# A transformer block with exact fp32 products: the FFN's down products taken from three float32r matmuls, and each FFN sum completed inside one PSUM bank

## The chip, the cores and the metric

The kernel runs on one core of a Trainium2 chip. The time is that of one execution on the device, in microseconds (us). A core has five engines that run side by side, each working through its own queue in order: TensorE (PE) multiplies matrices, VectorE (DVE) and ScalarE (ACT) work element by element, GpSimd (POOL) does the same on SBUF alone, and SyncE (SP) issues the DMAs. Matmul results land in PSUM, which has eight banks of 128 x 512 fp32.

## What is computed

One block over x of 2048 tokens x 512 features: a layer norm, causal attention with 16 heads of 32, and a gated feed-forward network (FFN) of width 4096 on the same normalized input. The FFN's weights are 4-bit codes with a scale for each block of 32.

```python
xn = layernorm(x)
# attention: qkv, causal softmax, output projection with w_o
Wg, Wu, Wd = dequant(gate), dequant(up), dequant(down)
gate, up = xn @ Wg.T, xn @ Wu.T              # 2048 x 4096 each
gelu = tanh(0.7978845608 * (gate + 0.044715 * gate**3)) * gate * 0.5 + gate * 0.5
out = x + attention(xn) + (gelu * up) @ Wd.T
```

## The kernel before

Attention comes first and takes about 855 us. Then the output projection adds into sixteen fp32 accumulators `acc` (128 tokens x 512), and the same loop splits the normalized tokens `xnT` for the FFN. Then the FFN runs.

*Splitting.* A float32r matmul is made exact by cutting each fp32 number into a high part (its upper bits, taken with a mask, `HIGH`) and the low rest. A product of two split numbers is the sum of high x high, low x low and one "mixed" matmul, whose operands are `high * SPLIT - low` on each side; the constants `HIGH_SCALE` and `MIXED_SCALE` bring the sums together. `TRUE` undoes the scale that the decoding of codes leaves.

*Weights.* The FFN's 4096 rows are handled as 8 groups `g` of 4 chunks `j` of 128 rows. For every chunk there are three pieces of weights: gate (m = 0), up (m = 1) and half of a down pair (m = 2). `load_words` (L553) loads the codes and scales of a piece with one DMA and eight DMAs on SP's queue. `piece` (L571) decodes it: five VectorE passes of 128 x 256 (L582 to L600) and two GpSimd multiplies by the scales. For a down piece (L601) that is all: the result goes straight to the fp32 tiles `wd`. A gate or up piece is then split: a VectorE mask for `high` (L625), a GpSimd subtraction for the low part (L626), two ScalarE passes (L627, L628) and a second GpSimd subtraction (L629). This second half, the "rest", is handed out only after the next piece's first four steps.

*Who hands it out.* `weights` (L649) is a generator over all pieces; each `yield` carries an estimate in us. `advance(us)` (L677) takes steps until its budget is spent, `need` (L686) takes steps until a tile exists, and `limit` says how many pieces may have been made so far. So the order on VectorE, GpSimd and ScalarE is fixed by where `advance` and `need` are called. Every engine works in the order in which the code issues; `tc.manual_schedule()` keeps it.

*FFN slots.* The loop at L833 runs over g, j and the four token blocks b in the order 1, 2, 3, 0: 128 slots. `gate_and_up` (L785) makes in each slot twelve matmuls for gate and twelve for up (`products`, L770: high, low and mixed for each of four k), each sum in two PSUM banks. `combine` (L765) copies one bank with a scale to SBUF on ScalarE and adds the other on VectorE. ScalarE applies the gelu, VectorE multiplies gate and up into `inter`. After each of the two groups of twelve, `down` (L809) takes one tile of 128 tokens from a list and adds two fp32 matmuls for it, over the chunks j - 1 and j. An fp32 matmul shows as two MATMUL records. `add` (L825) adds the result to `acc` on VectorE with the factor `TRUE`. The list is filled after every second chunk, so down products trail by up to eight slots, and the `inter` tiles have ten buffers.

*Buffers.* `xnT` of all token blocks is one pool (`norm`) on the right side of SBUF, closed before the FFN. The FFN's pools on the left are, in order, `lm` (split tokens), `acc`, `wd`, `stage`, `deq`, `gu`. The output projection's weights `wo` use two of the four `gu` tiles. A tile that is put where an older one lay waits for that one's last reader.

Of the kernel before, what the change touches and what calls it, by code (L numbers as in the profile page):

```python
# [34 lines left out]
BF16 = mybir.dt.bfloat16  # L36
# [29 lines left out]
HIGH_SCALE = (1.0 + SPLIT) * TRUE  # L66
MIXED_SCALE = -TRUE / SPLIT
# [7 lines left out]
def block_kernel(  # L75
# [12 lines left out]
    const = ctx.enter_context(tc.tile_pool(name="const", bufs=1))  # L88

    ident = const.tile([P, P], F32, tag="ident", name="ident")  # L90
    make_identity(nc, ident)

    mask_qk = const.tile([P, TB], F32, tag="mask_qk", name="mask_qk")
    nc.vector.memset(mask_qk[:, : TB - P], 0.0)
    make_causal_mask(nc, mask_qk[:, TB - P :], mask_val=MASKED)
    ident_h = const.tile([P, P], BF16, tag="ident_h", name="ident_h")
    nc.vector.tensor_copy(ident_h, ident)
    ones_h = const.tile([P, P], BF16, tag="ones_h", name="ones_h")
    nc.vector.memset(ones_h, 1.0)
    ones = const.tile([P, D], F32, tag="ones", name="ones")  # L100
    nc.vector.memset(ones, 1.0)

# [6 lines left out]
    norm_stack = ExitStack()  # L109
    norm = norm_stack.enter_context(tc.tile_pool(name="norm", bufs=1, side="right"))  # L110

    xnT = [norm.tile([P, NK, TB], F32, tag=f"xnT{b}", name=f"xnT{b}") for b in range(NTB)]


    with (
        tc.manual_schedule(),
        tc.tile_pool(name="small", bufs=4) as small,
# [11 lines left out]
    ):  # L129

# [410 lines left out]
    wdp = ctx.enter_context(tc.tile_pool(name="wd", bufs=2, reuse_waits="tile"))  # L541
# [27 lines left out]
    gu, wd = {}, {}  # L569

    def piece(g, m, j, staged):  # L571

        key = f"{g}_{m}_{j}"
        pk, sc = staged  # L580
        code = tp.tile([P, W], I32, tag="code", name=f"code{key}")
        nc.vector.tensor_scalar(code, pk, 0xFF, None, ALU.bitwise_and)  # L582
        yield 0.29
        spread = tp.tile([P, W], I32, tag="spread", name=f"spread{key}")
        nc.vector.scalar_tensor_tensor(
            spread, code, 12, code, ALU.logical_shift_left, ALU.bitwise_or
        )
# [12 lines left out]
        nc.vector.tensor_tensor(mag, y, spread, ALU.bitwise_or)  # L600
        if m == 2:  # L601

            cols = slice((j % 2) * W, (j % 2 + 1) * W)
            for nib in range(2):
                c = 2 * (j // 2) + nib
                if (g, c) not in wd:
                    wd[g, c] = wdp.tile([P, H], F32, tag=f"wd{nib}", name=f"wd{g}_{c}")
                codes = mag16.rearrange("p (n nib) -> p nib n", nib=2)[:, nib]
                nc.gpsimd.tensor_tensor(wd[g, c][:, cols], codes, sc, ALU.mult)
            yield 0.43  # L610
            return

        w = tp.tile([P, NK, P], F32, tag="w", name=f"w{key}")
        for c in range(2):
            nc.gpsimd.tensor_tensor(  # L615
                w[:, 2 * c : 2 * c + 2],
                mag16.rearrange("p (c n nib) -> p c nib n", c=2, nib=2)[:, c],
                sc[:, :P].unsqueeze(1).to_broadcast([P, 2, P]),
                ALU.mult,
            )  # L620
        yield 0.43
        yield None
        parts = gup.tile([P, 3, NK, P], F32R, tag="gu", name=f"gu{key}")
        high = tp.tile([P, NK, P], F32, tag="high", name=f"high{key}")
        nc.vector.tensor_scalar(high.bitcast(I32), w.bitcast(I32), HIGH, None, ALU.bitwise_and)  # L625
        nc.gpsimd.tensor_tensor(parts[:, 1], w, high, ALU.subtract)  # L626
        nc.scalar.activation(parts[:, 2], high, AF.Copy, scale=SPLIT)  # L627
        nc.scalar.copy(parts[:, 0], high)  # L628
        nc.gpsimd.tensor_tensor(  # L629
            parts[:, 2], parts[:, 2].bitcast(F32), parts[:, 1].bitcast(F32), ALU.subtract  # L630
        )
        gu[g, m, j] = parts
        yield 0.43


    pieces = [(0, 0, 0), (0, 1, 0), (0, 2, 0)]
    for g in range(NG):
        for j in range(0, NC, 2):
            pieces += [(g, 0, j + 1), (g, 1, j + 1), (g, 2, j + 1)]
            h, i = (g, j + 2) if j + 2 < NC else (g + 1, 0)  # L640
            if h < NG:
                pieces += [(h, 0, i), (h, 1, i), (h, 2, i)]
# [6 lines left out]
    def weights():  # L649
# [3 lines left out]
        while True:  # L653
            if made < limit[0]:
# [11 lines left out]
                if key[1] < 2:  # L666
                    rest = ops
# [7 lines left out]
    budget, limit = [0.0], [3]  # L675
# [43 lines left out]
    with tc.manual_schedule():  # L719
# [15 lines left out]
        for n, t in enumerate(order):  # L735
# [13 lines left out]
            if n >= 4:  # L749
                token_high(ORDER[n // 4 - 1], n % 4)  # L750
            if n >= 3:
# [5 lines left out]
        norm_stack.close()  # L757


        ip = ctx.enter_context(  # L760
            tc.tile_pool(name="inter", bufs=10, side="right", reuse_waits="tile")
        )
        ep = ctx.enter_context(tc.tile_pool(name="elem", bufs=2, side="right", reuse_waits="tile"))

        def combine(ps, dst, name):  # L765
            t = ep.tile([P, TB], F32, tag="t", name=f"t{name}")
            nc.scalar.activation(t, ps[0], AF.Copy, scale=HIGH_SCALE)  # L767
            nc.vector.scalar_tensor_tensor(dst, ps[1], MIXED_SCALE, t, ALU.mult, ALU.add)  # L768

        def products(g, m, j, b):  # L770

            ps = [bank(f"gu{g}_{m}_{j}_{b}_{i}") for i in range(2)]
            parts = gu[g, m, j]
            for k in range(NK):
                for dst, i, mov, start, stop in (
                    (ps[0], 0, xh[b, k], k == 0, False),
                    (ps[0], 1, lm[b][:, 0, k], False, k == NK - 1),
                    (ps[1], 2, lm[b][:, 1, k], k == 0, k == NK - 1),
                ):
                    nc.tensor.matmul(dst, lhsT=parts[:, i, k], rhs=mov, start=start, stop=stop)  # L780
            return ps

        inters = {}

        def gate_and_up(g, j, b):  # L785
            name = f"{g}_{j}_{b}"
            need(lambda: (g, 0, j) in gu and (g, 1, j) in gu)
            ps = products(g, 0, j, b)
            down()
            gate = ep.tile([P, TB], F32, tag="gate", name=f"gate{name}")  # L790
            combine(ps, gate, f"g{name}")
            nc.scalar.activation(gate, gate, AF.Gelu_apprx_tanh)
            advance(0.5)
            add()
            ps = products(g, 1, j, b)
            down()
            advance(0.8)
            inter = ip.tile([P, TB], F32, tag="inter", name=f"inter{name}")
            combine(ps, inter, f"u{name}")
            nc.vector.tensor_tensor(inter, gate, inter, ALU.mult)  # L800
            inters[g, j, b] = inter
            if j % 2 == 1:
                downs.extend((g, j, 4 * b + i) for i in range(4))
            add()
            advance(1.4)

        downs, adds = [], []

        def down():  # L809

            if not downs:
                return
            g, j, t = downs.pop(0)
            po = bank(f"pd{g}_{j}_{t}")
            for c in (j - 1, j):
                nc.tensor.matmul(  # L816
                    po,
                    lhsT=inters[g, c, t // 4][:, (t % 4) * P : (t % 4 + 1) * P],
                    rhs=wd[g, c],
                    start=(c == j - 1),  # L820
                    stop=(c == j),
                )
            adds.append((g, j, t, po))

        def add():  # L825
            if not adds:
                return
            g, j, t, po = adds.pop(0)
            nc.vector.scalar_tensor_tensor(acc[t], po, TRUE, acc[t], ALU.mult, ALU.add)  # L829
            if (g, j) == (NG - 1, NC - 1):  # L830
                nc.sync.dma_start(out=out[t * P : (t + 1) * P, :], in_=acc[t])
# [6 lines left out]
        while downs:  # L838
            down()
            add()  # L840
# [53 lines left out]
```

## Time and profile before

| | |
|---|---|
| median of 3 runs | 2074.04 us (2071.06 to 2079.86) |
| the profiled execution | 2072.73 us, span 2071.0 us |
| TensorE busy in the span | 2034.8 us |
| VectorE, ScalarE, GpSimd busy | 1174.1, 740.6, 451.3 us |
| mean granted TensorE clock | 0.998 of full |
| gate and up matmuls (L780), 3072 | 640.0 + 503.3 us busy |
| down matmuls (L816), 1024 records | 479.6 us busy |

The spans of neighbouring matmuls overlap, since a matmul starts before the one before it has drained. Busy time of a group therefore counts shared time once for one of them, and a matmul's "mean ns" is longer than its place in the queue; the distance from start to start is what it costs. The clock is granted in steps of half and full speed.

### The profile page before, as it was taken

How to read it: one execution, taken by the hardware profiler on the slowest of the kernel's cores; microseconds unless marked ns; L12 is line 12 of the kernel's file. 1: busy time of each engine (PE TensorE's matmuls, PEld its weight loads, DVE VectorE, ACT ScalarE, POOL GpSimd, SP SyncE). 2: the span in 40 equal slices, each digit the busy share in tenths (PEclk: the TensorE clock that was granted, in tenths of full speed). 3: DMA queues.
4: the chain of work that ended last, by engine and by line, in shares of the span. 5: the costliest groups of instructions: out<-in, count | busy, mean ns of one | idle time of the engine just before them, and what ended most of it. 6: DMA issues, size and time to landing. Idle time of an engine off the chain costs nothing.

```text
span 2071.0 us, 28569 instructions
## 1 busy us (share of the span) xinstructions
PE 2034.8 (98%) x10560; PEld 1067.8 (52%) x10560; DVE 1174.1 (57%) x2354; ACT 740.6 (36%) x1624; POOL 451.3 (22%) x700
## 2 busy tenths in 40 slices
PE   7999999999999999999999999999999999999999
PEld 3433233332333222356666666666666666666665
DVE  5657665557555730496556465555556565555553
ACT  2113565456545577423222222222222222222221
POOL 0000021111111120353323122232313222232310
PEclk9999999999999999999999999999999999999999
DMA  3000000000000000300000000000000000000002
GB/s 122 0 11 31 1 1 1 1 1 1 1 1 1 2 2 1 97 14 26 22 16 21 16 20 20 20 20 17 22 17 18 19 20 19 20 20 16 21 3 81
DMA packets 54941, 39.63 MB, mean 19 GB/s; under 512 B 14737, under 2 KB 47505, under 8 KB 54673
## 3 DMA queue, kind: packets, MB, share of 16 engines
q1 hardware_dynamic: 54800, 37.81, 6.2%
q8 instruction: 83, 1.36, 0.3%
q14 instruction: 58, 0.47, 0.1%
HBM read 33.55 MB, written 4.19 MB: 18 GB/s over the span
## 4 chain that ended last, share of the span: by engine, by line
PE 93%; DVE 3%; ACT 2%; issue 1%; POOL 1%; DMA 0%; DVEq 0%; POOLq 0%; ACTq 0%
PE gu L780 33%; PE pd L816 21%; PE av L342 12%; PE ps_s L205 9%; PE ps_qk L161 6%; PE ps_t L279 4%; PE ps_t L294 3%; PE ps_v L444 3%; ACT prob L308 1%; PE po L738 1%; PE pm L260 0%; POOL lm L705 0%; PE ptx L433 0%; DVE highx L704 0%; DVE sums L362 0%
## 5 line engine op out<-in xcount | busy, mean ns | idle before, releaser
L780 PE MATMUL gu<-lm,gu 128*128 128x512 f32 x2048 | 640.0, 393 | 2.3 <-DVE gate L768 1.2
L780 PE MATMUL gu<-xh,gu 128*128 128x512 f32 x1024 | 503.3, 491 | 1.2 <-ACT tg L767 1.2
L816 PE MATMUL pd<-wd,inter 128*128 128x512 f32 x1024 | 479.6, 592 | 0.6 <-DVE inter L800 0.6
L780 PEld LDWEIGHTS gu<-lm,gu 128*128 128x128 f32 x2048 | 385.1, 188 | 141.3 <-issue 59.3
L229 DVE TENSOR_REDUCE tops<-ps_s 128x1 f32<-128x512 f32 x384 | 243.8, 682 | 157.3 <-PE ps_s L205 137.1
L342 PE MATMUL av<-prob,v 128*32 128x512 f32 (+3 forms) x1280 | 290.3, 542 | 3.7 <-DVE sums L362 2.8
L205 PE MATMUL ps_s<-qk,qk 32*128 32x512 f32 (+3 forms) x1280 | 291.2, 576 | 0.0
L342 PE MATMUL av<-prob,ones 128*32 128x512 f32 (+3 forms) x1280 | 290.3, 542 | 0.0
L816 PEld LDWEIGHTS pd<-wd,inter 128*128 128x128 f32 x1024 | 193.7, 189 | 149.1 <-issue 128.2
L294 PE MATMUL ps_t<-qk,qk 32*128 32x512 f32 (+3 forms) x1280 | 263.6, 535 | 0.0
L308 ACT ACTIVATE prob<-ps_t 128x512 f32<-128x512 f32 x384 | 205.8, 597 | 154.5 <-PE ps_t L294 153.2
L780 PEld LDWEIGHTS gu<-xh,gu 128*128 128x128 f32 x1024 | 192.8, 188 | 94.1 <-issue 58.6
L768 DVE SCALAR_TENSOR_TENSOR gate<-gu,tg 128x512 f32<-128x512 f32 x128 | 88.5, 691 | 231.5 <-ACT tg L767 231.4
L615 POOL TENSOR_TENSOR w<-mag,sc 128x256 f32<-128x256 f16 x128 | 98.2, 788 | 541.9 <-DVE mag L600 541.9
L768 DVE SCALAR_TENSOR_TENSOR inter<-gu,tu 128x512 f32<-128x512 f32 x128 | 88.5, 691 | 218.8 <-ACT tu L767 218.8
L767 ACT ACTIVATE tg<-gu 128x512 f32<-128x512 f32 x128 | 76.1, 594 | 358.5 <-PE gu L780 358.5
L829 DVE SCALAR_TENSOR_TENSOR acc<-pd,acc 128x512 f32<-128x512 f32 x256 | 175.4, 685 | 41.2 <-PE pd L816 41.2
L224 DVE CUSTOM_DVE_ANT_0 ps_s<-ps_s,mask_qk 128x128 f32<-128x128 f32 (+3 forms) x256 | 120.8, 517 | 100.2 <-PE ps_t L294 55.7
L767 ACT ACTIVATE tu<-gu 128x512 f32<-128x512 f32 x128 | 76.3, 596 | 269.8 <-PE gu L780 269.8
L342 PEld LDWEIGHTS av<-prob,v 128*32 128x32 f32 x1280 | 49.4, 108 | 200.9 <-issue 160.2
L319 POOL TENSOR_SCALAR_AFFINE_SELECT prob<-prob 128x256 f32<-128x256 f32 x128 | 52.0, 406 | 432.3 <-ACT prob L318 385.6
L626 POOL TENSOR_TENSOR gu<-w,high 128x512 fp32r<-128x512 f32 x64 | 85.6, 1337 | 238.7 <-DVE high L625 236.3
(75 smaller groups left out, 1965.0 us busy)
## 6 DMA issues: line engine op xcount, KB each, us to landing
pk<-packed SPq DMA_DIRECT2D x96, 128.0 KB, 2.1
sc<-scales SPq DMA_DIRECT2D x512, 8.0 KB, 1.6
x<-x SPq DMA_DIRECT2D x16, 256.0 KB, 3.5
acc<-x SPq DMA_DIRECT2D x16, 256.0 KB, 4.1
sc<-scales SPq DMA_DIRECT2D x256, 16.0 KB, 1.7
out<-acc SPq DMA_DIRECT2D x16, 256.0 KB, 2.0
wqk<-w_qk SPq DMA_DIRECT2D x4, 512.0 KB, 3.6
wv<-w_v SPq DMA_DIRECT2D x1, 1024.0 KB, 6.7
```

The costliest lines, as they stand in the source:

```text
L161: nc.tensor.matmul(ps, lhsT=w[:, k, which, :], rhs=xnT[b][:, k, :], start=(k == 0), stop=(k == NK - 1),)
L205: nc.tensor.matmul(ps[:, :w], lhsT=qT[p // 2, qb][rows, i * P : (i + 1) * P], rhs=kT[p // 2, c][rows, :w], start=True, stop=True,)
L224: nc.vector.tensor_tensor_reduce(ps[:, :w], ps[:, :w], mask_qk[:, TB - w :], 1.0, MASKED, ALU.add, ALU.max, top,)
L229: nc.vector.tensor_reduce(top, ps[:, :w], AX.X, ALU.max)
L294: nc.tensor.matmul(ps[:, c0:], lhsT=kT[p // 2, kt // 4][rows, (kt % 4) * P : (kt % 4 + 1) * P], rhs=qT[p // 2, qb][rows, c0:], start=False ...
L308: nc.scalar.activation(prob[:, h, :], ps, AF.Exp)
L342: nc.tensor.matmul(av[D * h : D * (h + 1), c0:], lhsT=v[kt // 4][:, kt % 4, D * head : D * (head + 1)] if h < 2 else ones, rhs=prob[:, h % ...
L767: nc.scalar.activation(t, ps[0], AF.Copy, scale=HIGH_SCALE)
L768: nc.vector.scalar_tensor_tensor(dst, ps[1], MIXED_SCALE, t, ALU.mult, ALU.add)
L780: nc.tensor.matmul(dst, lhsT=parts[:, i, k], rhs=mov, start=start, stop=stop)
L816: nc.tensor.matmul(po, lhsT=inters[g, c, t // 4][:, (t % 4) * P : (t % 4 + 1) * P], rhs=wd[g, c], start=(c == j - 1), stop=(c == j),)
L829: nc.vector.scalar_tensor_tensor(acc[t], po, TRUE, acc[t], ALU.mult, ALU.add)
```

## The change

1. A down piece is split like a gate or up piece. Its tile `wd` now holds three float32r parts for a pair of chunks; a last ScalarE pass scales the low part (`ready` counts the finished halves of a pair). The list of pieces is made anew: down pieces are made one pair ahead.
2. The down product of a slot's `inter` is made for that chunk alone, in the next slot: `inter` is split into three parts, then for each of four token tiles two matmuls (high, low), a ScalarE rescale of the bank in place, and later one mixed matmul into the same bank. VectorE adds the bank to `acc`, now four times a slot.
3. Gate and up sums use one bank each: eight matmuls, a ScalarE rescale in place, then four mixed matmuls into it. `combine` goes; the gelu and the multiplication read PSUM with a scale.
4. `advance` is called once a slot, with 2.2, where it was called with 0.5, 0.8 and 1.4.
5. Pools: `const` closes with attention, `norm` becomes four pools that close one by one, and `wd` opens only when two of them have.

```diff
-HIGH_SCALE = (1.0 + SPLIT) * TRUE
-MIXED_SCALE = -TRUE / SPLIT
+HIGH_SCALE = -(1.0 + SPLIT) * SPLIT
+SUM_SCALE = -TRUE / SPLIT
...
-    wdp = ctx.enter_context(tc.tile_pool(name="wd", bufs=2, reuse_waits="tile"))
...
+        if m == 2:
+            pair = (g, j // 2)
+            if pair not in wd:
+                wd[pair] = wdp[0].tile([P, 2, 3, H], F32R, tag="wd", name=f"wd{g}_{j // 2}")
+                ready[pair] = 0
+            cols = slice((j % 2) * W, (j % 2 + 1) * W)
+            parts = [wd[pair][:, :, i, cols] for i in range(3)]
+            w, high = (t.rearrange("p (c k) n -> p c (k n)", c=2) for t in (w, high))
+        else:
+            gu[g, m, j] = gup.tile([P, 3, NK, P], F32R, tag="gu", name=f"gu{key}")
+            parts = [gu[g, m, j][:, i] for i in range(3)]
+        nc.gpsimd.tensor_tensor(parts[1], w, high, ALU.subtract)
+        nc.scalar.activation(parts[2], high, AF.Copy, scale=SPLIT)
+        nc.scalar.copy(parts[0], high)
         nc.gpsimd.tensor_tensor(
-            parts[:, 2], parts[:, 2].bitcast(F32), parts[:, 1].bitcast(F32), ALU.subtract
+            parts[2], parts[2].bitcast(F32), parts[1].bitcast(F32), ALU.subtract
         )
         yield 0.43
+        if m == 2:
+            nc.scalar.activation(parts[1], parts[1].bitcast(F32), AF.Copy, scale=1.0 / SPLIT)
+            ready[pair] += 1
...
+    pieces = [(0, 0, 0), (0, 1, 0), (0, 2, 0), (0, 2, 1)]
+    for n in range(NG * NC):
+        g, j = divmod(n + 1, NC)
+        if g < NG:
+            pieces += [(g, 0, j), (g, 1, j)]
+        g, j = divmod(2 * (n // 2 + 1) + n % 2, NC)
+        if g < NG:
+            pieces.append((g, 2, j))
...
-                if key[1] < 2:
-                    rest = ops
+                rest = ops
...
+        def high_and_low(g, m, j, b):
+            ps = bank(f"gu{g}_{m}_{j}_{b}")
+            parts = gu[g, m, j]
+            for k in range(NK):
+                for i, mov in ((0, xh[b, k]), (1, lm[b][:, 0, k])):
+                    nc.tensor.matmul(ps, lhsT=parts[:, i, k], rhs=mov, ...)
+            nc.scalar.activation(ps, ps, AF.Copy, scale=HIGH_SCALE)
+            return ps
+        def mixed(g, m, j, b, ps):
+            for k in range(NK):
+                nc.tensor.matmul(ps, lhsT=gu[g, m, j][:, 2, k], rhs=lm[b][:, 1, k], start=False, ...)
+        def gate_and_up(g, j, b, finish):
+            need(lambda: (g, 0, j) in gu and (g, 1, j) in gu)
+            gate_sum = high_and_low(g, 0, j, b)
+            up_sum = high_and_low(g, 1, j, b)
+            mixed(g, 0, j, b, gate_sum)
+            gate = ep.tile([P, TB], F32, tag="gate", name=f"gate{name}")
+            nc.scalar.activation(gate, gate_sum, AF.Gelu_apprx_tanh, scale=SUM_SCALE)
+            next(finish, None)
+            advance(2.2)
+            mixed(g, 1, j, b, up_sum)
+            inter = ep.tile([P, TB], F32, tag="inter", name=f"inter{name}")
+            nc.vector.scalar_tensor_tensor(inter, up_sum, SUM_SCALE, gate, ALU.mult, ALU.mult)
+            parts = ip.tile([P, 3, TB], F32R, tag="parts", name=f"parts{name}")
+            high = ep.tile([P, TB], F32, tag="hi", name=f"hi{name}")
+            nc.vector.tensor_scalar(high.bitcast(I32), inter.bitcast(I32), HIGH, None, ALU.bitwise_and)
+            nc.scalar.copy(parts[:, 0], high)
+            nc.gpsimd.tensor_tensor(parts[:, 1], inter, high, ALU.subtract)
+            next(finish, None)
+            return down(g, j, b, parts, high)
+        def down(g, j, b, parts, high):
+            nc.vector.scalar_tensor_tensor(
+                parts[:, 2], high, SPLIT, parts[:, 1].bitcast(F32), ALU.mult, ALU.subtract
+            )
+            need(lambda: ready.get((g, j // 2)) == 2)
+            w = wd[g, j // 2][:, j % 2]
+            sums = []
+            for i in range(4):
+                po = bank(f"pd{g}_{j}_{b}_{i}")
+                for part in range(2):
+                    nc.tensor.matmul(po, lhsT=parts[:, part, i * P : (i + 1) * P], rhs=w[:, part], ...)
+                nc.scalar.activation(po, po, AF.Copy, scale=HIGH_SCALE)
+                sums.append(po)
+            yield
+            for i, po in enumerate(sums):
+                nc.tensor.matmul(po, lhsT=parts[:, 2, i * P : (i + 1) * P], rhs=w[:, 2], start=False, ...)
+                t = 4 * b + i
+                nc.vector.scalar_tensor_tensor(acc[t], po, SUM_SCALE, acc[t], ALU.mult, ALU.add)
...
         for g in range(NG):
             for j in range(NC):
                 for b in ORDER:
-                    limit[0] = min(3 * (NC * g + j + 2), 3 * NC * NG)
-                    gate_and_up(g, j, b)
+                    limit[0] = min(4 + 3 * (NC * g + j + 1), 3 * NC * NG)
+                    finish = gate_and_up(g, j, b, finish)
```

The generator `finish` holds the down product of the slot before: its first `next` issues the split's last part, the eight matmuls and the rescales, its second the mixed matmuls and the accumulations.

More of the change, by code (lines that the diff above doesn't have):

```diff
@@ L108, in block_kernel @@
     ]
[L109 to L112 removed]
+    norms, xnT = {}, {}
+    for b in reversed(ORDER):
+        norms[b] = ExitStack()
+        norm = norms[b].enter_context(tc.tile_pool(name=f"norm{b}", bufs=1, side="right"))
+        xnT[b] = norm.tile([P, NK, TB], F32, tag="xnT", name=f"xnT{b}")
     with (
         tc.manual_schedule(),
+        tc.tile_pool(name="const", bufs=1) as const,
         tc.tile_pool(name="small", bufs=4) as small,
@@ L610, in piece @@
[L610 to L620, printed above, removed]
+                nc.gpsimd.tensor_tensor(
+                    w[:, 2 * nib : 2 * nib + 2].rearrange("p k n -> p (k n)"), codes, sc, ALU.mult
+                )
+        else:
+            for c in range(2):
+                nc.gpsimd.tensor_tensor(
+                    w[:, 2 * c : 2 * c + 2],
+                    mag16.rearrange("p (c n nib) -> p c nib n", c=2, nib=2)[:, c],
+                    sc[:, :P].unsqueeze(1).to_broadcast([P, 2, P]),
+                    ALU.mult,
+                )
@@ L621, in piece @@
         yield 0.43
         yield None
-        parts = gup.tile([P, 3, NK, P], F32R, tag="gu", name=f"gu{key}")
         high = tp.tile([P, NK, P], F32, tag="high", name=f"high{key}")
         nc.vector.tensor_scalar(high.bitcast(I32), w.bitcast(I32), HIGH, None, ALU.bitwise_and)
-        nc.gpsimd.tensor_tensor(parts[:, 1], w, high, ALU.subtract)
-        nc.scalar.activation(parts[:, 2], high, AF.Copy, scale=SPLIT)
-        nc.scalar.copy(parts[:, 0], high)
+        if m == 2:
[6 more added lines that the diff above has]
+            w, high = (t.rearrange("p (c k) n -> p c (k n)", c=2) for t in (w, high))
+        else:
+            gu[g, m, j] = gup.tile([P, 3, NK, P], F32R, tag="gu", name=f"gu{key}")
+            parts = [gu[g, m, j][:, i] for i in range(3)]
@@ L674, in block_kernel @@
     work = weights()
-    budget, limit = [0.0], [3]
+    budget, limit = [0.0], [2]
     def advance(us):
@@ L756, in block_kernel @@
             token_high(ORDER[-1], k)
[L757 to L768, printed above, removed]
@@ L770, in products @@
-        def products(g, m, j, b):
-            ps = [bank(f"gu{g}_{m}_{j}_{b}_{i}") for i in range(2)]
+        for b in ORDER[2:]:
+            norms[b].close()
+        ep = ctx.enter_context(tc.tile_pool(name="elem", bufs=1, side="right", reuse_waits="tile"))
+        ip = ctx.enter_context(tc.tile_pool(name="ip", bufs=2, side="right", reuse_waits="tile"))
+        def high_and_low(g, m, j, b):
+            ps = bank(f"gu{g}_{m}_{j}_{b}")
             parts = gu[g, m, j]
             for k in range(NK):
[L775 to L780, printed above, removed]
-            return ps
@@ L783, in block_kernel @@
-        inters = {}
-        def gate_and_up(g, j, b):
+                for i, mov in ((0, xh[b, k]), (1, lm[b][:, 0, k])):
+                    nc.tensor.matmul(
+                        ps,
+                        lhsT=parts[:, i, k],
+                        rhs=mov,
+                        start=(k == 0 and i == 0),
+                        stop=(k == NK - 1 and i == 1),
+                    )
+            nc.scalar.activation(ps, ps, AF.Copy, scale=HIGH_SCALE)
+            return ps
+        def mixed(g, m, j, b, ps):
+            for k in range(NK):
+                nc.tensor.matmul(
+                    ps,
+                    lhsT=gu[g, m, j][:, 2, k],
+                    rhs=lm[b][:, 1, k],
+                    start=False,
+                    stop=(k == NK - 1),
+                    skip_group_check=True,
+                )
@@ L793, in gate_and_up @@
[L793 to L807, printed above, removed]
@@ L816, in down @@
                 nc.tensor.matmul(
                     po,
[L818 to L821, printed above, removed]
-                )
[L823 to L831, printed above, removed]
+                    lhsT=parts[:, 2, i * P : (i + 1) * P],
@@ L833, in block_kernel @@
+                    rhs=w[:, 2],
+                    start=False,
+                    stop=True,
+                    skip_group_check=True,
+                )
+                t = 4 * b + i
+                nc.vector.scalar_tensor_tensor(acc[t], po, SUM_SCALE, acc[t], ALU.mult, ALU.add)
+                if (g, j) == (NG - 1, NC - 1):
+                    nc.sync.dma_start(out=out[t * P : (t + 1) * P, :], in_=acc[t])
+        finish = iter(())
         for g in range(NG):
@@ L835, in block_kernel @@
                 for b in ORDER:
-                    limit[0] = min(3 * (NC * g + j + 2), 3 * NC * NG)
-                    gate_and_up(g, j, b)
-        while downs:
-            down()
-            add()
+                    limit[0] = min(4 + 3 * (NC * g + j + 1), 3 * NC * NG)
+                    finish = gate_and_up(g, j, b, finish)
+        for _ in finish:
+            pass
 def _arranged(a):
```

68 lines of the change are left out of this document (32 added, 36 removed).

## The prediction

> **What bounds the kernel now.** I read the page's table of engines first, then the chain of waits in the feed-forward part, then single instructions there.
>
> ```profile
> PE 2034.8 (98%) x10560; PEld 1067.8 (52%) x10560; DVE 1174.1 (57%) x2354; ACT 740.6 (36%) x1624; POOL 451.3 (22%) x700
> ```
>
> TensorE (PE) is full and nothing else is near it. The chain of waits over 20 us of the feed-forward part, in order of time (start, length, what):
>
> ```profile
> by line: PE gu L780 62.5%; PE pd L816 38.6%
> ...
> 1403.11 2.78 PE gu L780 x12
> 1405.88 1.72 PE pd L816 x4
> 1407.60 2.78 PE gu L780 x12
> 1410.38 1.72 PE pd L816 x4
> ```
>
> No other engine is on the chain. Twelve float32r matmuls take 2.78 us, 0.232 each; the four records of two fp32 down matmuls take 1.72, so 0.86 for each fp32 matmul. One slot (a chunk j and token block b) is 2 x 4.50 = 9.0 us, and 128 slots are 1152 us of the 2071. Only what changes TensorE's work, or makes it wait, counts. Now the other engines over one weight piece (start, length, engine, line; a bracket is idle time before it):
>
> ```profile
> 1416.53 1.35 POOL L626 TENSOR_TENSOR gu<-w,high 128x512 fp32r<-128x512 f32 x1 [5.72 <-DVE high L625]
> ...
> 1417.96 1.29 POOL L629 TENSOR_TENSOR gu<-gu 128x512 fp32r<-128x512 f32 x1
> 1418.07 1.46 DVE L585 SCALAR_TENSOR_TENSOR spread<-code 128x256 int32<-128x256 int32 x1
> ...
> 1422.40 0.42 DVE L625 TENSOR_SCALAR high<-w 128x512 int32<-128x512 int32 x1
> ...
> 1422.85 0.63 ACT L627 ACTIVATE gu<-high 128x512 fp32r<-128x512 f32 x1 [3.03 <-DVE high L625]
> 1422.96 1.33 POOL L626 TENSOR_TENSOR gu<-w,high 128x512 fp32r<-128x512 f32 x1 [2.16 <-DVE high L625]
> 1423.39 0.61 ACT L628 CAST gu<-high 128x512 fp32r<-128x512 f32 x1
> ...
> 1424.38 1.27 POOL L629 TENSOR_TENSOR gu<-gu 128x512 fp32r<-128x512 f32 x1
> 1425.61 1.43 POOL L609 TENSOR_TENSOR wd<-mag,sc 128x256 f32<-128x256 f16 x2
> ```
>
> ScalarE (ACT) passes are 0.6 us and start 0.53 apart when queued; GpSimd (POOL) steps are 1.3 us, a pair of scale multiplies 1.43; VectorE (DVE) hands to POOL after about 0.13. Last, TensorE's clock where it was idle: windows of 3.41 us, with its busy time first and the granted clock third from the end:
>
> ```profile
> 840.83:844.25 3.42, 1.48 (x15) 0.48 (x12) 0.52 (x1) 3.38 (x11) 0.81 (x2) 1.00 0.00 0
> 844.25:847.66 3.41, 3.09 (x16) 0.68 (x16) 3.35 (x5) 2.48 (x10) 1.37 (x4) 0.50 0.00 0
> 851.08:854.49 3.41, 1.63 (x28) 0.47 (x24) 1.07 (x2) 2.35 (x7) 1.84 (x5) 1.00 0.38 118
> 854.49:857.90 3.41, 3.04 (x4) 1.49 (x5) 3.38 (x5) 0.00 (x0) 1.31 (x3) 0.50 0.08 19
> ...
> 936.41:939.82 3.41, 2.17 (x9) 1.31 (x8) 0.86 (x3) 2.65 (x6) 3.33 (x4) 1.00 0.16 41
> 939.82:943.24 3.42, 3.42 (x17) 2.78 (x16) 2.20 (x4) 1.82 (x4) 0.51 (x1) 1.00 0.15 39
> ```
>
> Busy for 1.48 or 1.63 of 3.41 us, the next window has half the clock (four fp32 records start in the second, where about eight do at full clock); busy for 2.17, it keeps it.
>
> **The sum of matmuls.** Out go 512 fp32 matmuls: 512 x 0.86 = 440. In come 3 x 4 per slot, 1536 float32r matmuls of the shape of the gate and up ones: 1536 x 0.232 = 356. Gate and up keep their 24. Term: -84 us (bounds -78 and -88, a pitch 0.004 off). A slot becomes 36 x 0.232 = 8.35 us: gate pairs until 1.86, up pairs 3.71, gate mixed 4.64, eight matmuls of the previous slot's down product 6.50, up mixed 7.42, its four mixed ones 8.35.
>
> **Work on the other engines, per slot.** ACT: the two copies with scale become rescales in place (0.6 each), the gelu stays, four rescales of down sums and one copy of `high` come in, 0.6 each; with 7 weight passes per four slots (4 before) about 5.9 of 8.35 us. DVE: two combines and a product (2.1) become one product, one mask and one mixed part (0.69 + 0.42 + 0.78), and accumulations go from two to four (+1.37); with weights about 6.6. POOL: one subtraction (1.34) per slot, and two more per down piece; about 4.5. Each sum fits under 8.35, so by load alone TensorE would hide it all. Down's rescales and weight passes stand in queues, though, so I followed the order in which the new code issues them. DMAs of weights stay: 96 pieces, the same bytes.
>
> **Where the queue does not fit.** Per chunk, three weight pieces are spread by the budget of 2.2 per slot. The third slot (b = 3) draws, in this order: the rest of the up piece, the scale multiplies of the down piece, and at once the down piece's own rest, ending in a rescale of its low part. ACT, all in issue order, has behind that rescale the copy of `parts[:, 0]` and then the next slot's gate rescale, for which TensorE waits. Times from the slot's first matmul:
> - gelu starts when the gate mixed matmuls have drained (4.64 + 0.19; a matmul takes 0.40 at a pitch of 0.23) = 4.83; four down rescales start at 5.39, 5.92, 6.45, 6.98; the up piece's `high x SPLIT` pass runs 7.51 to 8.13.
> - POOL's second subtraction of that piece needs it: 8.25 to 9.54. Only then come the down piece's multiplies, 9.50 to 10.93.
> - DVE's mask `high`: 10.97 to 11.39. POOL's subtractions: 11.53 to 12.86 and 12.95 to 14.24.
> - ACT's rescale of the low part reads what the second subtraction reads, so it waits for it: 14.28 to 14.88; copy, start 14.81; gate rescale 15.35 to 15.95; TensorE goes on at 16.0.
>
> TensorE reached that point at 8.35 + 3.71 = 12.06. It waits 3.9 us. DVE meanwhile holds this slot's product behind the blocked mask (from 7.4 to about 11.3), but the down matmuls that need it come later than the gate ones. In the other three slots the same ledger leaves over 1 us at each gate rescale, and about 1 us where the down matmuls wait for POOL's subtraction, so nothing is added.
>
> The last two chunks have no down piece left to make: 30 stalls x 3.9 = +117. Bounds: with in-place PSUM rescales at 0.72 (the in-place DVE pass L224, 717 ns against 682 for one that only reads) each of five grows 0.12: 4.5. With POOL at the longest L629 (1.60) and multiplies at 1.86 (L609 at 902.49), four steps grow by some 1.4: 5.3. Without hand-over delays: 3.4. I keep 3.9, as most of L629 is at its median of 1.29.
>
> **The clock.** A gap of 3.9 us laid over a grid of 3.41 leaves, at any phase, one window with at most 3.41 - 1.95 = 1.46 us of work. By the rows above that halves the next. Laying the gap at all phases with a limit of 1.75 (between 1.63 and 2.17), a stall loses 0.8 to 2.4 us of TensorE time, 1.5 on average: 30 x 1.5 = +45. Nothing hides this, since TensorE is the bound again after the stall. Bounds 0 and 72.
>
> The Trainium skill speaks differently here (TensorE: Matmul & The Clock Gate, Part 1): the half clock comes after at least one idle window of about 3.4 us. A 3.9 us gap holds a whole window in about one phase of seven, so by the page this term would be near 6 and the time near 2127; the two rows halved with over 1.4 us of work in them, so I go by them.
>
> **Start and end.** The weights output (`wo`) moves: with the pool of `wd` gone from ahead of it, its buffers lie on those of `sums`, so its four DMAs on SP's queue wait for POOL's late normalizations (one ends at 853.4 in this trace) and all loads of `acc`, words and scales queue behind them. Landing takes 3.5 us (DMA view), against a start of the output projection at 854.9: +2 to +4, up to 7.4 if the wait is for the last normalization at 858.8; I take +4. The first chunk must make two down pieces before the second slot's down product, and POOL spends 4 us on each: 0 to 10, I take 3. At the end the last product goes mask, subtraction, eight matmuls, rescales, four matmuls, accumulation, uncovered: 2.8 us until its first matmuls less 0.9 of cover, plus about 1 for the rescales: +3.
>
> Sum: 2073 (profiled execution, 2071 span; the median is 2074) - 84 + 117 + 45 + 4 + 3 + 3 = 2161. **Forecast: 2161 us, slower by 4.2%.**
>
> **Rivals.**
> - *Matmuls alone decide (faster).* If the chain in the third slot ends 3.9 us sooner, say because ACT's rescale need not wait for POOL's subtraction and POOL runs the multiplies first, the time is 2073 - 84 + 10 = 1999. For it: every engine's load is under 80% of 8.35. Against: POOL and ACT take instructions in order in all rows above. It decides below 2.5 us of stall plus clock per chunk (74/30).
> - *Stall without clock.* 2161 - 45 = 2116. For it: the halved windows held narrow matmuls (32 columns), so full ones may count for more.
> - *POOL stretched.* Where POOL and DVE overlap, both grow (L585 1.46 against 0.43 alone); at 5.3 us per stall the time is 2161 + 30 x 1.4 = 2203, and later waits for POOL's subtraction could add some.
> - *The change does not do what it says:* float32r down matmuls at a pitch nearer fp32's. Against: 3072 of the same shape run at 0.232.
>
> **How the numbers follow.** Forecast 0.62, its own range 2135 to 2190; without clock 0.17; stretched 0.12; matmuls alone 0.09, of which 0.02 is spread over no change. A measurement of this kernel tells about 0.5% from no change. So faster 0.07, same 0.02, slower 0.91. The range runs 2100 to 2207: it leaves out the faster side and the far end of the stretched one.
>
> **What would show it.** Down matmuls at 0.232; one wait of about 3.9 us on ACT per four slots, before the gate's mixed matmuls of the block after b = 3; half-clock windows after it; TensorE near 90% busy. Equal waits in all four slots, or none, would make the ledger wrong; waits without halved windows, the clock term.

## The result, and the profile after

| | before | after |
|---|---|---|
| median | 2074.1 us (2071.1 to 2079.9) | 2180.2 us (2179.3 to 2183.9, 4 runs) |
| ratio | | 1.0516 (95%: 1.0499 to 1.0533) |
| span of the profiled execution | 2071.0 us | 2177.4 us |
| mean granted clock | 0.998 | 0.961 |

The kernel became 5.2% slower. The forecast was 2161 us, slower by 4.2%, with 2100 to 2207 as its range.

The page of the changed kernel, in its table of engines, its chain and its costliest group:

```profile
PE 2024.2 (93%) x11072; PEld 1207.7 (55%) x11072; DVE 1345.6 (62%) x2642; ACT 1118.9 (51%) x2360; POOL 705.0 (32%) x892
PE 71%; ACT 8%; POOL 7%; issue 5%; SPq 3%; DVE 3%; DMA 2%; POOLq 0%; DVEq 0%; ACTq 0%
L803 PE MATMUL gu<-lm,gu 128*128 128x512 f32 x1024 | 310.1, 429 | 114.7 <-ACT gu L797 114.7
```

TensorE is busy for 11 us less although the matmuls that went should have saved 84; part of its busy time now runs at half clock. 153 us of the span it is idle, where it was 36 before. The chain of work has ScalarE and GpSimd on it (8% and 7%), although they are busy for only 51% and 32% of the span: they are not full, they are late. Nearly all of the new idle time stands before one line, the mixed matmuls L803, and ends with ScalarE's rescale L797. TensorE's waits by line, with total us, times and longest:

```profile
PE gu L803 <- ACT gu L797: 114.7, 31, 10.3
```

Thirty-one waits: one of 10.3 us, in the first slot of the FFN, twenty-nine of 3.53, in the last slot (b = 0) of each chunk from the second to the thirtieth, and one of 1.95 near the end (2121.09). One of the twenty-nine as it comes about, on the timeline (start, length, engine, line; the bracket is idle time before it and what ended it). The third slot's first matmul starts at 1408.70:

```profile
1414.06 2.06 ACT L856 ACTIVATE pd<-pd 128x512 f32<-128x512 f32 x4
1416.00 0.65 ACT L635 ACTIVATE gu<-high 128x512 fp32r<-128x512 f32 x1
1416.79 1.29 POOL L637 TENSOR_TENSOR gu<-gu 128x512 fp32r<-128x512 f32 x1 [1.45 <-ACT gu L635]
...
1418.04 1.43 POOL L607 TENSOR_TENSOR w<-mag,sc 128x256 f32<-128x256 f16 x2
...
1419.51 0.43 DVE L622 TENSOR_SCALAR high<-w 128x512 int32<-128x512 int32 x1 [5.32 <-POOL w L607]
...
1420.02 1.29 POOL L634 TENSOR_TENSOR wd<-w,high 128x512 fp32r<-128x512 f32 x1 [0.54 <-DVE high L622]
1421.39 1.33 POOL L637 TENSOR_TENSOR wd<-wd 128x512 fp32r<-128x512 f32 x1
1422.75 0.63 ACT L642 ACTIVATE wd<-wd 128x512 fp32r<-128x512 f32 x1 [1.64 <-POOL wd L637]
1423.28 0.60 ACT L833 CAST parts<-hi 128x512 fp32r<-128x512 f32 x1
...
1423.79 1.06 ACT L797 ACTIVATE gu<-gu 128x512 f32<-128x512 f32 x2
...
1424.42 2.08 PE L803 MATMUL gu<-lm,gu 128*128 128x512 f32 x4 [3.53 <-ACT gu L797]
```

Read it from below. TensorE waits for L797; L797 stands in ScalarE's queue behind L833 and L642; L642 waits for GpSimd's second subtraction of the down piece; that piece was late because GpSimd took its multiplies (L607) only after the up piece's subtraction L637, and that one waited for ScalarE's pass L635, which stood behind the four down rescales L856. The brackets show how each engine of the row waits for another one (1.45, 5.32, 0.54, 1.64, 3.53): the row is a chain through three queues, and none of them is loaded.

What the stall does to the clock, in windows of 3.41 us (TensorE's busy time is the first figure after the length, the granted clock the third from the end):

```profile
1420.00:1423.41 3.41, 0.89 (x4) 0.37 (x2) 3.38 (x6) 1.77 (x4) 3.32 (x3) 1.00 0.13 34
1423.41:1426.83 3.42, 2.41 (x6) 1.95 (x7) 1.26 (x2) 1.68 (x4) 0.54 (x1) 0.50 0.03 5
1426.83:1430.24 3.41, 3.41 (x10) 2.67 (x9) 0.00 (x0) 2.40 (x5) 0.00 (x0) 0.50 0.00 0
1430.24:1433.65 3.41, 3.41 (x16) 2.76 (x15) 2.47 (x5) 0.91 (x2) 1.20 (x1) 1.00 0.00 0
...
1460.96:1464.37 3.41, 0.15 (x1) 0.15 (x2) 3.41 (x6) 1.83 (x4) 2.70 (x3) 1.00 0.14 31
1464.37:1467.79 3.42, 3.42 (x9) 2.65 (x10) 0.10 (x1) 1.46 (x3) 0.00 (x0) 0.50 0.00 0
```

A window with 0.89 us of work halves the next. That next one holds the rest of the stall and so 2.41 us of work, and it halves one more. At another phase (second group) nearly all of the stall lies in one window, and only the next is halved. In a full window at half clock 9 or 10 matmuls are under way at some time, at full clock 16.

### The profile page after: what moved, and what is told of

It is laid out like the page before. It is cut to its first block, busy times and chain, and to the rows that moved or that the text cites. A ratio compares the mean times of both kernels' runs of the same rounds, so it can differ in the third digit from the quotient of the medians.

```text
span 2177.4 us, 31084 instructions
## 1 busy us (share of the span) xinstructions
PE 2024.2 (93%) x11072; PEld 1207.7 (55%) x11072; DVE 1345.6 (62%) x2642; ACT 1118.9 (51%) x2360; POOL 705.0 (32%) x892
## 3 DMA queue, kind: packets, MB, share of 16 engines
q8 instruction: 87, 1.43, 0.3%
## 4 chain that ended last, share of the span: by engine, by line
PE 71%; ACT 8%; POOL 7%; issue 5%; SPq 3%; DVE 3%; DMA 2%; POOLq 0%; DVEq 0%; ACTq 0%
PE gu L790 13%; PE av L344 11%; PE gu L803 10%; PE ps_s L207 8%; PE pd L849 8%; PE ps_qk L163 6%; PE ps_t L281 4%; PE pd L860 3%; PE ps_t L296 3%; SPq L567 3%; PE ps_v L446 3%; ACT pd L856 2%; POOL w L607 2%; POOL wd L637 2%; DMA pk<-packed 2%
## 5 line engine op out<-in xcount | busy, mean ns | idle before, releaser
L803 PE MATMUL gu<-lm,gu 128*128 128x512 f32 x1024 | 310.1, 429 | 114.7 <-ACT gu L797 114.7
L790 PE MATMUL gu<-xh,gu 128*128 128x512 f32 x1024 | 403.6, 394 | 0.0
L790 PE MATMUL gu<-lm,gu 128*128 128x512 f32 x1024 | 400.7, 391 | 0.0
L869 DVE SCALAR_TENSOR_TENSOR acc<-pd,acc 128x512 f32<-128x512 f32 x512 | 316.7, 678 | 0.7 <-PE pd L860 0.7
L803 PEld LDWEIGHTS gu<-lm,gu 128*128 128x128 f32 x1024 | 208.4, 206 | 176.3 <-ACT gu L797 128.3
L849 PE MATMUL pd<-wd,parts 128*128 128x512 f32 x1024 | 296.5, 438 | 4.2 <-ACT wd L636 1.8
L856 ACT ACTIVATE pd<-pd 128x512 f32<-128x512 f32 x512 | 268.7, 582 | 23.9 <-PE pd L849 23.9
L834 POOL TENSOR_TENSOR parts<-inter,hi 128x512 fp32r<-128x512 f32 x128 | 165.6, 1294 | 332.1 <-DVE hi L830 332.1
L849 PEld LDWEIGHTS pd<-wd,parts 128*128 128x128 f32 x1024 | 221.3, 216 | 61.7 <-ACT wd L636 2.2
L826 DVE SCALAR_TENSOR_TENSOR inter<-gu,gate 128x512 f32<-128x512 f32 x128 | 88.3, 690 | 253.4 <-PE gu L803 246.5
L797 ACT ACTIVATE gu<-gu 128x512 f32<-128x512 f32 x256 | 145.7, 577 | 177.5 <-PE gu L790 177.5
L790 PEld LDWEIGHTS gu<-lm,gu 128*128 128x128 f32 x1024 | 192.3, 188 | 42.8 <-issue 0.2
```

Source lines behind the costliest of these rows:

```text
L790: nc.tensor.matmul(ps, lhsT=parts[:, i, k], rhs=mov, start=(k == 0 and i == 0), stop=(k == NK - 1 and i == 1),)
L797: nc.scalar.activation(ps, ps, AF.Copy, scale=HIGH_SCALE)
L803: nc.tensor.matmul(ps, lhsT=gu[g, m, j][:, 2, k], rhs=lm[b][:, 1, k], start=False, stop=(k == NK - 1), skip_group_check=True,)
L834: nc.gpsimd.tensor_tensor(parts[:, 1], inter, high, ALU.subtract)
L849: nc.tensor.matmul(po, lhsT=parts[:, part, i * P : (i + 1) * P], rhs=w[:, part], start=(part == 0), stop=(part == 1),)
L856: nc.scalar.activation(po, po, AF.Copy, scale=HIGH_SCALE)
```

## The experiments

Two questions were open: does the order in ScalarE's queue make the stall (and not the load of the engines, or a slower matmul), and what part of the loss is the clock? Each run stood beside the kernel before on the same chip (2073.6 us for the first four, 2072.8 for the last two).

**e1: the down piece's rest leaves the third slot.** With a smaller budget the rest of the down piece (L622 to L642) is drawn whole in the next slot, b = 0, where no other rest is due. No work is added or removed.

```diff
-            advance(2.2)
+            advance(1.9)
```

> The changed kernel with a weight budget of 1.9 instead of 2.2 per slot: the same instructions, but the down piece's split (mask, two subtractions, three ScalarE passes) is now issued in the fourth slot (b = 0) instead of the third. Queue theory (ScalarE's rescale of the low part waits for GpSimd in the third slot, and the gate rescale stands behind it): the 30 waits of about 3.5 us go, and with them the halved clock windows; 2180 - 104 - about 70 = 2000 to 2012 us. Load theory (GpSimd and VectorE are too busy or slow each other, wherever the work is put): the waits move to another slot and the time stays within 20 us of 2180.

Measured: 2009.65 us (2008.8 to 2010.6), ratio to before 0.9695 (0.968 to 0.9709), clock 0.993. TensorE waits for L797 twice, 12.3 us in all, the longest 10.4. ScalarE's timeline in a slot b = 0, where the down piece now is:

```profile
1428.66 0.65 ACT L635 ACTIVATE wd<-high 128x512 fp32r<-128x512 f32 x1
...
1430.78 0.63 ACT L642 ACTIVATE wd<-wd 128x512 fp32r<-128x512 f32 x1 [0.96 <-POOL wd L637]
1431.32 0.60 ACT L833 CAST parts<-hi 128x512 fp32r<-128x512 f32 x1
1431.83 0.58 ACT L797 ACTIVATE gu<-gu 128x512 f32<-128x512 f32 x1
1433.58 0.58 ACT L797 ACTIVATE gu<-gu 128x512 f32<-128x512 f32 x1 [1.17 <-PE gu L790]
```

The twenty-nine stalls are gone, and with them the halved windows that followed them. The wait of 1.95 us is still there, as in e2, e3, e4 and e6: it stands in a slot b = 3 in which the last up piece is split and no down piece is left. L642 waits for GpSimd 0.96 us instead of 1.64 and ends soon enough: the second L797 waits for TensorE again, not the other way round. By load there is room for all the new work, as VectorE (68%), ScalarE (55%) and GpSimd (35%) show. The changed kernel is so 3.1% faster than the one before instead of 5.2% slower, by one constant.

**e2: only L642 leaves.** With a budget of 2.0 the down piece's masks and subtractions stay in the third slot, and only the last step, ScalarE's rescale of the low part, moves on.

```diff
-            advance(2.2)
+            advance(2.0)
```

> Budget 2.0: of the down piece only the last ScalarE pass (low part rescaled) moves to the fourth slot; the multiplies, mask and subtractions stay in the third. Queue theory: the gate rescale no longer waits for the second subtraction, only for the two passes behind the mask, so the wait is about 1.6 us, and the down matmuls behind it wait some 0.6 for the late subtraction; fewer windows are halved: 2060 to 2110 us. Load theory: no change from 2180.

Measured: 2109.41 us (2108.3 to 2114.1), ratio 1.0183 (1.0166 to 1.02), clock 0.978. TensorE waits 31 times for L797, 69.1 us in all, the longest 10.4. The third slot on the timeline:

```profile
1392.69 0.43 DVE L622 TENSOR_SCALAR high<-w 128x512 int32<-128x512 int32 x1 [4.99 <-POOL w L607]
1393.04 0.68 DVE L826 SCALAR_TENSOR_TENSOR inter<-gu,gate 128x512 f32<-128x512 f32 x1
...
1393.76 1.02 DVE L830 TENSOR_SCALAR hi<-inter 128x512 int32<-128x512 int32 x1
...
1394.86 0.62 ACT L833 CAST parts<-hi 128x512 fp32r<-128x512 f32 x1 [0.57 <-DVE hi L830]
1395.39 1.06 ACT L797 ACTIVATE gu<-gu 128x512 f32<-128x512 f32 x2
```

With L642 gone from the slot the next thing on the same road comes to light: L833 needs VectorE's L830, and VectorE has the product L826 behind the mask L622, which waits for GpSimd's multiplies. The stall is now (69.1 - 10.4) / 30 = 1.96 us, so L642's wait made some 1.5 us of 3.5, and the mask that was waited for in order the other 2. In 0.57 of these ScalarE waits for L830, which takes 1.02 us here, beside GpSimd's L634 and L637, and 0.43 where GpSimd is idle. The time is at the upper edge of what was expected, since the stall was put at 1.6. That the loss comes from the number of passes is out: the passes are the same in all three kernels.

This run also brackets where the clock falls:

```profile
1505.48:1508.89 3.41, 1.48 (x6) 1.15 (x7) 3.38 (x6) 1.98 (x5) 2.99 (x3) 1.00 0.13 34
1508.89:1512.31 3.42, 3.42 (x9) 2.68 (x9) 0.38 (x1) 2.61 (x6) 0.00 (x0) 0.50 0.02 5
...
1689.80:1693.21 3.41, 1.65 (x7) 1.29 (x8) 3.40 (x6) 1.98 (x5) 2.81 (x3) 1.00 0.12 30
1693.21:1696.63 3.42, 3.42 (x17) 2.77 (x16) 1.15 (x3) 2.73 (x6) 0.00 (x0) 1.00 0.00 0
```

With 1.48 us of work the next window is halved, with 1.65 it is not; the lowest after one of these stalls that was not followed by half clock had 1.58 (2020.89 to 2024.30), and one at the start of the FFN had 1.53 (914.97 to 918.39). This holds for these windows, not everywhere: at the end of the changed kernel 1.77 us of the last down matmuls (2170.92 to 2174.33) were followed by half clock.

**e3: the stall filled with matmuls.** Fifteen matmuls of the gate's shape go to a spare bank before the gate's mixed ones in every slot b = 0; nobody reads their result. They cost TensorE what the wait costs it, but keep it busy: what is left of the loss against the changed kernel is the clock.

```diff
             up_sum = high_and_low(g, 1, j, b)
+            if b == 0:
+                spare = bank(f"fill{name}")
+                for i in range(15):
+                    nc.tensor.matmul(spare, lhsT=gu[g, 0, j][:, 0, i % NK], rhs=xh[b, i % NK], start=True, stop=True)
             mixed(g, 0, j, b, gate_sum)
```

> The changed kernel with 15 more float32r matmuls into a spare bank before the gate's mixed matmuls of each fourth slot (b = 0); nobody reads their result. They take 3.5 us, which is the wait. Clock theory (TensorE's idleness halves the next windows and this costs about 74 us): clock back to about 1.0, time 2180 - 70 = about 2110, although the wait itself is as long and TensorE has 111 us more work. Rival (the halved windows cost little, the wait is everything): 2175 to 2195.

Measured: 2135.83 us (2131.4 to 2137.8), ratio 1.03 (1.0285 to 1.0316), clock 0.995. So 44 us came back by adding work. But 2110 was expected, and 26 us are missing. Fifteen fillers take 3.76 us from their start (1402.39) to the mixed matmuls (1406.15), about what the wait takes, not less; and they also stand in the three chunks that have no such stall, the first and the last two, for some 10 us. That left a doubt about the rest, hence e6.

**e6: thirteen fillers, and none in the last two chunks.**

```diff
-            if b == 0:
+            if b == 0 and NC * g + j < 30:
...
-                for i in range(15):
+                for i in range(13):
```

> As the filled kernel, with 13 matmuls instead of 15 and only in the 30 chunks that have the wait, so that they end before it does and add nothing. Clock theory: what is gained against the changed kernel is the clock's price alone, 60 to 70 us: 2110 to 2120. If the filled kernel's 45 us were all of it: 2130 to 2140.

Measured: 2124.54 us (2121.2 to 2125.4), ratio 1.0243 (1.0226 to 1.026), span 2123.4, clock 0.994. The timeline of one filled stall:

```profile
1403.43 3.19 PE L822 MATMUL fill<-xh,gu 128*128 128x512 f32 x13
...
1407.17 1.20 PE L803 MATMUL gu<-lm,gu 128*128 128x512 f32 x4 [0.55 <-ACT gu L797]
```

The fillers are too few by 0.55 us, so the stall stands in its full length, 1407.17 - 1403.43 = 3.74 us in TensorE's queue, and at full clock. (The profile's idle time is shorter by what the last matmul takes to drain.) The span is 54.0 us below the changed kernel's and 114.5 above e1's. In this stand also 3.0 us of fillers in the first chunk, which has no stall to fill (it lasts 51.74 us, 48.78 in the changed kernel), and an FFN that starts at 913.6 where the changed kernel's starts at 912.0. Cleaner is the length of a chunk, from its first matmul to that of the next; here three successive starts in the changed kernel, then two in e6, then two in e1:

```profile
1392.02 0.40 PE L790 MATMUL gu<-xh,gu 128*128 128x512 f32 x1
1431.80 0.40 PE L790 MATMUL gu<-xh,gu 128*128 128x512 f32 x1
1470.52 0.40 PE L790 MATMUL gu<-xh,gu 128*128 128x512 f32 x1
...
1411.94 0.40 PE L790 MATMUL gu<-xh,gu 128*128 128x512 f32 x1
1449.16 0.40 PE L790 MATMUL gu<-xh,gu 128*128 128x512 f32 x1
...
1396.33 0.40 PE L790 MATMUL gu<-xh,gu 128*128 128x512 f32 x1
1429.69 0.40 PE L790 MATMUL gu<-xh,gu 128*128 128x512 f32 x1
```

A chunk of the changed kernel lasts 39.78 or 38.72 us in turn, with two halved windows or one; a chunk of e6 lasts 37.22, one of e1 33.36. The twenty-nine chunks with the stall take 1137.9, 1079.3 and 967.4 us: 59 us are the clock and 112 the stall. e6 is 4.5 us over the expected 2120 because the clock had been priced at 60 to 70 and the first chunk's fillers at nothing. The same two things, 11 us of clock and 10 of fillers, are most of the 26 that e3 lacked.

**e4: the first slot's sums before the last tokens.** In all these kernels a first wait of 10.4 us is left. e4 is e1 with the first slot's sixteen gate and up matmuls and both rescales issued before the last token passes.

```diff
+        early = [sums_of(0, 0, ORDER[0])]
         end(tokens)
         for k in range(NK):
             token_high(ORDER[-1], k)
...
-            gate_sum = high_and_low(g, 0, j, b)
-            up_sum = high_and_low(g, 1, j, b)
+            gate_sum, up_sum = early.pop() if early else sums_of(g, j, b)
```

> As with the budget of 1.9, and the first slot's sixteen gate and up matmuls with their two rescales issued before the last token passes, so that these rescales don't stand behind them on ScalarE. Queue theory of the start: of the first wait of 10.3 us some 5 to 8 go, and a halved window or two with it: 5 to 10 us below the kernel with the budget of 1.9 alone. Rival: the first wait is for data (the last tokens), not for the queue: no difference.

Measured: 2010.02 us (2008.7 to 2012.7), ratio 0.9698 (0.9684 to 0.9712): nothing gained on e1. Its timeline at the start:

```profile
923.10 0.63 ACT L723 ACTIVATE lm<-lm 128x512 fp32r<-128x512 f32 x1 [2.15 <-DVE lm L720]
923.63 1.06 ACT L788 ACTIVATE gu<-gu 128x512 f32<-128x512 f32 x2
924.27 3.78 PE L808 MATMUL gu<-lm,gu 128*128 128x512 f32 x8 [7.57 <-ACT gu L788]
...
928.35 1.28 ACT L825 ACT_TABLE_LOAD   x1 [1.82 <-DVE xh L728]
```

The first wait is shorter (7.57), since one token pass less (L723) stands ahead of the rescale L788; the ones before it still do. Waits of 1.14, 1.77 and 1.50 us follow. The first gelu, whose table load it is, still waits for VectorE's last token pass L728, and the down sums for the second down piece. The expectation was wrong: past one token pass the sums come sooner, but what follows them does not. The gelu reads nothing that L728 makes, so its wait is likely one for a buffer; that is not shown, nor what a rescale ahead of all token passes would gain.

**e5: the other half of the change alone.** The kernel before with the one-bank sums for gate and up (eight matmuls, rescale in place, four mixed ones), its down products and weights untouched.

```diff
+            nc.scalar.activation(ps, ps, AF.Copy, scale=HIGH_SCALE)
+            return ps
+        def mixed(g, m, j, b, ps):
...
-            combine(ps, gate, f"g{name}")
-            nc.scalar.activation(gate, gate, AF.Gelu_apprx_tanh)
+            nc.scalar.activation(gate, gate_sum, AF.Gelu_apprx_tanh, scale=SUM_SCALE)
```

> The kernel before with one part of the change alone: gate and up sums in one bank each, eight matmuls, ScalarE's rescale in place, four mixed matmuls; the gelu and the product read PSUM. Down products, weights and budgets stay as before. Queue theory: no long wait stands in ScalarE's queue here, so TensorE hides the rescales: the slot stays 9.0 us and the time within 10 us of 2074 (the start may lose up to 10, since the first mixed matmuls now wait for a rescale behind the last token passes). Rival (the rescale between the matmuls of a sum is itself what TensorE waits for): some 0.5 us for each of 256 sums, 2150 to 2200.

Measured: 2080.55 us (2078.6 to 2082.1), ratio 1.0036 (1.0023 to 1.0049). Its only waits of TensorE in the FFN:

```profile
PE gu L784 <- ACT gu L778: 8.6, 2, 7.0
```

In 126 of 128 slots TensorE does not wait for the rescale at all. That matmuls need a result of ScalarE in the middle of a sum is thus no loss by itself; it makes TensorE depend on ScalarE's queue being short at that moment. Of the 7.7 us that it is above the kernel before, 5.7 lie in the first two chunks (65.9 us against 60.2), where both waits stand; each later chunk lasts 36.00 us instead of 35.95.

## Why the prediction was right, and which terms were off

*Matmuls, -84: right.* The third slot, shown above, starts at 1408.70 and the next one at 1417.04: 8.34 us, where 8.35 was forecast. A chunk of e1 lasts 33.36 us, one of the kernel before 35.95: 32 x 2.59 = 83. (The bound -88 is a slip: 0.004 more or less for each of 1536 matmuls is 6 us, so -78 and -90.)

*The stall's place and road: right in every step.* The ledger from the slot's first matmul against the trace (start minus 1408.70): first down rescale 5.39 and 5.36, up piece's pass 7.51 and 7.30, second subtraction 8.25 and 8.09, multiplies 9.50 and 9.34, mask 10.97 and 10.81, the down piece's subtractions 11.53 and 11.32, 12.95 and 12.69, its rescale 14.28 and 14.05, gate rescale 15.35 and 15.09, TensorE 16.0 and 15.72. All rows are early by about 0.2, since queued rescales start 0.49 apart (four in 2.06) where 0.53 was taken. The forecast counted 30 stalls; 29 of this kind came, as the first chunk has none. So the +117 are 29 x 3.86 = 112 (e6's chunks against e1's), of which 3.7 each is the wait itself. e1 and e2 show the road by cutting it: without the rest, no stall; without L642 alone, half of one.

*The clock, +45: there, but too small.* The changed kernel's chunks against e6's: 59, or 2.0 a stall where 1.5 was taken. The step that was mis-sized is "laying the gap at all phases with a limit of 1.75": after these stalls the limit lay between 1.48 and 1.58, and the forecast halved one window for each dip. But a window at half clock with 2.4 us of work leaves the one after it at half clock too, and 14 of the 29 stalls took two windows. That second window was not in the forecast. (The 1.63 us that did halve in the kernel before were matmuls of 32 columns, and 1.77 did at the end of the changed kernel, so busy time is not the whole measure.) The Trainium skill's rule (TensorE: Matmul & The Clock Gate, Part 1) that at least a whole idle window comes first does not describe these rows: windows with up to 1.48 us of work halved the next one, and by an estimate from the rule the term would have been near 6. (The sum would then be 2161 - 45 + 6 = 2122, not the 2127 that the prediction names.)

*The start, "I take 3": the term that was most off.* The forecast looked at the down pieces only. The waits that are there: 10.34 us of TensorE before the first mixed matmuls, then 1.77 and 1.07 for the second down piece. The first of them on the timeline of the changed kernel:

```profile
925.38 0.63 ACT L723 ACTIVATE lm<-lm 128x512 fp32r<-128x512 f32 x1 [2.15 <-DVE lm L720]
925.92 1.06 ACT L797 ACTIVATE gu<-gu 128x512 f32<-128x512 f32 x2
...
926.55 3.78 PE L803 MATMUL gu<-lm,gu 128*128 128x512 f32 x8 [10.34 <-ACT gu L797]
```

The first gate rescale is queued behind ScalarE's last token pass. Before, nothing on TensorE waited for ScalarE here for longer than 1.2 us, as gate and up had two banks each and needed no result in the middle. From the start of its first matmul to that of its last, the FFN of e1 takes 1089.8 us, 22 over its slots (128 x 8.34); before it was 4 (1155.7 against 1152). These are 18 more for start, end and leftovers, where the start's and the end's terms were 3 + 3. Some 12 of them are waits (13.2 at the start, 1.3 at the end and the one of 1.95, less 4.0 before). Around the waits of the start TensorE works 8.3 us in windows at half clock (926.96 to 933.78, 940.61 to 944.02), which by estimate cost some 4; the last 2 no run tells apart. e5 shows 5.7 us to come at the start with the one-bank sums. How to win it back stays open after e4.

*`wo`, +4:* TensorE waits 2.7 us for its DMA, as forecast, but at the same place it waited 1.5 us for VectorE before; the FFN's first matmul comes at 912.0 instead of 911.0: +1. *End, +3:* two waits, 1.09 and 0.24, and 5.2 us after the start of the last matmul where 4.3 were before: nearer 2.

Together: 2071 - 84 + 112 for the stall + 59 for the clock + 18 for start, end and leftovers + 1 for `wo` + 1 after the last matmul = 2178, against a span of 2177.4. By span the forecast was 2159, so 18 low: the clock 14 and the start with the end 13, less 5 for the stall and 3 for `wo`. The misses cancel in part, so the number is nearer than its terms.

*The rivals.* "Matmuls alone decide", 1999, is what e1 shows once its condition holds, plus the start. "Stall without clock", 2116, is e6's 2124.5, with 3.0 of fillers in its first chunk. "POOL stretched" did not come: GpSimd's steps on the road stayed at 1.29 to 1.33 and 1.43, though VectorE's passes beside them grew. The float32r down matmuls have the pitch of the others: eight of L849 take 2.03 us from 1413.31 on, 0.40 of it the last one's own.

## What to carry to other kernels

When a matmul sum needs a result of another engine in the middle, TensorE depends on what stands ahead of that result in that engine's queue; write that queue down in the order of issue, instruction by instruction, as load (51% here) says nothing of it. If such a stall comes every few slots, price the clock too, by laying the gap over the windows, and look whether moving one piece of work by a slot removes both: here one budget constant was worth 170 us. Draw the first slot separately: its queues hold what the stage before has left.

## What the runs showed of the hardware

After the FFN's stalls the granted clock fell where a window had up to 1.48 of 3.41 us of work and stayed from 1.58 on; at half clock, 2.4 us of work were too little to get it back for the next window. So a gap of 3.7 us cost another 2.0 us (59/29), and e3 and e6 became faster than the changed kernel by computing what nobody reads.

A VectorE pass on SBUF that ran beside a GpSimd pass took two to three times as long: in e2 the mask L830 took 0.43 us in the 65 cases with GpSimd idle and 1.01 to 1.28 in the 59 with GpSimd at work nearly all that time. The accumulation L869, which reads PSUM, took 0.68 either way. L830 with and without GpSimd's L637 beside it:

```profile
1373.59 0.43 DVE L830 TENSOR_SCALAR hi<-inter 128x512 int32<-128x512 int32 x1
...
1381.63 1.30 POOL L637 TENSOR_TENSOR gu<-gu 128x512 fp32r<-128x512 f32 x1 [2.27 <-ACT gu L635]
1381.93 1.28 DVE L830 TENSOR_SCALAR hi<-inter 128x512 int32<-128x512 int32 x1
```

Both are done within 0.3 us of each other. In the changed kernel this decided nothing, since L642 came later still; in the stall of e2 that is shown, it made ScalarE wait 0.57 us.

ScalarE's rescale in place in PSUM took 0.58 us (577 and 582 ns on average), where the copy from PSUM to SBUF before took 0.595; queued ones start 0.49 apart.
